# A chain of cross-attention layers on one core: another model behind the planned order, expert tiles in pairs, and zero rows written later

## Chip, core and metric

The kernel runs on one core of one Trainium2 chip. The metric is the device time of one execution in microseconds, as the median of several runs; less is better. A profile is one further execution, taken with the hardware profiler. The engines are TensorE (PE, matmuls and transposes; its weight loads are PEld), VectorE (DVE), ScalarE (ACT), GpSimd (POOL) and SyncE (SP, which here only issues transfers). ScalarE and GpSimd issue transfers too.

## What is computed

64 sequences of 128 x 128 float32 (`x`) and a context of 64 x 77 x 128 go through four layers. Layers 0 and 1 are single-head attentions without weight matrices (below called the front part). Layer 2 has self-attention, cross-attention with 16 heads of 8, and a mixture of experts; layer 3 has causal self-attention, cross-attention and a feed-forward part. Layer 2's experts are the part that the change touches:

```python
def _fuse_moe(x, ln_g, ln_b, rw, rb, fc1_w, fc1_b, fc2_w, fc2_b):   # E = 8, K = 2, DFF = 512
    h = _ln(x, ln_g, ln_b)
    logits = h @ rw.T + rb
    vals, idx = jax.lax.top_k(logits, K)
    gates = jax.nn.softmax(vals, axis=-1)
    hf = h.reshape(N, D)
    h1 = jax.nn.gelu(jnp.einsum('nd,efd->enf', hf, fc1_w) + fc1_b[:, None, :], approximate=False)
    eo = jnp.einsum('enf,edf->end', h1, fc2_w) + fc2_b[:, None, :]
    gathered = eo[idx_f, jnp.arange(N)[:, None], :]
    mixed = (gathered * gates_f[..., None]).sum(axis=1).reshape(x.shape)
    return x + mixed

x = _L0_xattn_ref(ctx_1024, x, ...)
x = _L1_xattn_ref(x, ctx_1024, ctx_1024, ...)
x = _L2_xattn_ref(x, ctx_1024, ...)
x = _L3_xattn_ref(x, ctx_1024, ...)
```

## The kernel before

**Tiles and sets.** The 64 sequences are taken four at a time: 16 batches, t = 0 to 15. Two batches (SG = 2, 1024 rows) make a set, of which there are 8. `front` (L974) does layers 0 and 1 of a batch, `middle` layer 2's two attentions, `router` the choice of two experts for each row, `dispatch` the places of a set's rows sorted by expert, and 16 scatters on GpSimd's queue (L1289) that write them into a DRAM tensor `sent[i]`. The rows of an expert fill whole tiles of 128, so a set has NT = 23 tiles, some rows of which no scatter writes. These must hold something finite, and so `sent[i]` is filled with zeros first (L700). `experts` reads the tiles in chunks of NL = 3 (7 chunks of 3 and one of 2), fetches each tile's expert weights by its number (L1326, L1327, on SP's queue, three buffers `we`, one tile ahead), and writes the answers to `answered[i]`. `gather` fetches each row's two answers (L1396), and `attention3` and `forward` do layer 3.

**An expert's tile.** One bf16 matmul with the bias parts and a mask (L1360), four float32 matmuls with the first weights (L1365), all into one PSUM tile `bank`; one Gelu on ScalarE over 128 x 512 (L1370); four matmuls with the second weights into another bank (L1375); and a copy on VectorE (L1376). ScalarE keeps one table of functions at a time. Gelu and Exp (L872, the softmaxes of the 16-head attentions) are in different ones, and the compiler puts an ACT_TABLE_LOAD between them.

**PSUM.** Three buffers `bank` (128 x 512 float32), used by nearly everything; one `banks` of four times that, for scores; one `po`, for the sums over keys.

**An attention tile.** Scores of one sequence into `banks` (L853 for the causal mask, L860); per half a maximum (L869) and a difference (L871) on VectorE and Exp on ScalarE (L872); eight transposes of the probabilities into two banks (L882), each copied by ScalarE (L883); sums over keys with narrow matmuls (L890), a copy (L941), a transpose (L899) and a division (L902, L903).

**The order.** It comes from two planners that run when the program is built. Each part above is a generator that yields before a piece of work the tiles that it needs. `Conductor` keeps a modelled time for each engine and lets that generator go on whose next piece can begin first (`begin`, with an age and a random blur from the plan; `ranks` break ties). The order of instructions so written is the program order, in which buffers are handed out. `Rehearsal` then takes all instructions with their dependencies and sorts those of TensorE, ScalarE, VectorE and GpSimd anew by a list schedule over modelled durations (`run`), and `apply` makes that order binding. In `run`, ScalarE puts off an instruction that would load a table by up to PATIENCE = 3000 ns if another is ready (`instead`). `run` also models TensorE's clock: in windows of WINDOW = 3413 ns it adds up TensorE's modelled work, and a window below a share BUSY makes the next one slow, with durations doubled. SP's queue keeps the program order. `tile_xattn_chain` rehearses each of four PLANS and builds the one with the least modelled length. A plan has a seed, the order in which an attention's four streams are added (`parts`), the batches that use the second of two lanes (`second`), the ranks, and a factor `slow` on TensorE's modelled time in `Conductor`. `Conductor` and `Rehearsal` each have a `cost` of their own.

**The start.** `load(0)` and `load(1)` on SP's queue; constants on ScalarE's queue (L579 to L601: columns, rows, fc1, fc2, matrices, router, biases, feed-forward weights); zeros for all eight sets on SP's queue (L690 to L701); and constants made on VectorE and TensorE (L615 onwards).

Of the kernel before, what the change touches and what calls it, by code (L numbers as in the profile page):

```python
# [40 lines left out]
    dict(age=2000.0, blur=300.0, seed=0, parts=(2, 3, 1, 0), second=(1, 3, 5), ranks=(2, 1, 0, 0, 0, 3), slow=1.2),  # L41
    dict(age=2000.0, blur=300.0, seed=527369, parts=(2, 0, 1, 3), second=(1, 3, 5), ranks=(2, 1, 0, 0, 2, 3), slow=1.2),
    dict(age=2000.0, blur=200.0, seed=622144, parts=(0, 1, 2, 3), second=(1, 3), ranks=(2, 1, 0, 0, 3, 3), slow=1.2),
    dict(age=2300.0, blur=200.0, seed=815169, parts=(3, 2, 0, 1), second=(1, 3), ranks=(2, 1, 0, 0, 0, 3), slow=1.2),
# [3 lines left out]
BUSY = (0.54, 0.88)  # L48
# [28 lines left out]

class Conductor:
# [7 lines left out]
    def __init__(self, block, bufs, plan):  # L86
        self.block, self.seen, self.bufs = block, 0, bufs
        self.age, self.blur, self.chance = plan["age"], plan["blur"], random.Random(plan["seed"])
        self.slow = plan["slow"]
        self.pe, self.table = 0.0, None  # L90
        self.busy, self.made, self.read, self.tiles = {}, {}, {}, {}
        self.streams = []
# [46 lines left out]
    def cost(self, i):  # L139

        kind = type(i).__name__
        sizes = [1.0]
        for o in list(i.ins) + list(i.outs):
            ap = getattr(o, "bass_ap", None)
            if ap is not None:
                size = 1.0
                for _, n in list(ap.ap)[1:]:
                    size *= n
                sizes.append(size)
        n, engine = max(sizes), i.engine.name  # L150
        if kind == "InstMatmult":
            n = sizes[1]
            if i.is_transpose:
                t = 0.85 * n
            elif "16" in str(i.ins[0].bass_ap.dtype):
                t = 0.43 * n
            else:
                t = 1.8 * n
            if i.tile_size is not None and 32 in tuple(i.tile_size):
                t *= 0.3  # L160
            return self.slow * t, self.slow * t + 160.0
        if "DMA" in kind:
            t = 950.0 if engine == "Pool" else 350.0
            return t, t + 2600.0
        if engine == "Pool":
            t = max(1000.0, 2.4 * n + 40.0)
            return t, t + 80.0
        if engine == "Activation":
            t = 80.0 + 0.83 * n
            if kind == "InstActivation":  # L170
                func = str(i.func)
                if "Exp" in func or "Gelu" in func:
                    if func != self.table:
                        t, self.table = t + 1283.0, func
                t += 100.0
            return t, t + 100.0
        t = 70.0 + 1.05 * n
        return t, t + 85.0

# [13 lines left out]
    def follow(self):  # L193

        instructions = self.block.instructions
        for i in instructions[self.seen :]:
            if "PoolBoundary" in type(i).__name__:
                continue
# [4 lines left out]
            for tensor in names[0]:  # L203
                t = max(t, self.made.get(tensor.name, 0.0))
            for tensor in names[1]:
                t = max(t, self.read.get(tensor.name, 0.0))
                tag = tensor.name.rsplit("_", 1)[0]
                if tag in self.bufs and tensor.name not in self.made:
                    t = max(t, self.free(tag))
                    self.tiles.setdefault(tag, []).append(tensor.name)  # L210
            keeps, takes = self.cost(i)
# [12 lines left out]
class Rehearsal:  # L224
# [3 lines left out]

    ENGINES = ("PE", "Activation", "DVE", "Pool")

    def __init__(self, block, slots):
        self.nodes = [i for i in block.instructions if "PoolBoundary" not in type(i).__name__]
# [59 lines left out]
    def cost(self, i, table):  # L292

        kind, engine, sizes, spaces, scalars = type(i).__name__, i.engine.name, [1], set(), 0
        aps = [[o.bass_ap for o in group if getattr(o, "bass_ap", None) is not None] for group in (i.ins, i.outs)]
        for ap in aps[0] + aps[1]:
            size = 1
            for _, n in list(ap.ap)[1:]:
                size *= n
            sizes.append(size)  # L300
            spaces.add(str(ap.tensor.space))
        n = max(sizes)
        scalars = sum(size == 1 for size in sizes[1:])
        if kind == "InstMatmult":
            n = sizes[1]
            if i.is_transpose:
                t = 0.85 * n
            elif "16" in str(aps[0][0].dtype):
                t = 0.42 * n
            else:  # L310
                t = 1.79 * n
            if i.tile_size is not None and i.tile_size[0] == 32:
                t = 0.237 * t + 30.0
            elif i.tile_size is not None and i.tile_size[1] == 32:
                t *= 0.315
            return t, t + 160.0, table
        if "DMA" in kind:
            t = 950.0 if engine == "Pool" else 360.0
            return t, t + 2600.0, table
        if engine == "Pool":  # L320
            t = 990.0 + 0.5 * n
            return t, t + 40.0, table
        if engine == "Activation":
            t = 165.0 + 0.833 * n
            if kind == "InstActivation":
                t += 90.0 * min(scalars, 2)
                func = str(i.func)
                if ("Exp" in func or "Gelu" in func) and func != table:
                    t, table = t + 1283.0, func
            return t - 98.0, t, table  # L330
        t = 150.0 + 1.04 * n + 60.0 * min(scalars, 2)
        if kind in ("InstTensorScalarPtr", "InstTensorCopy") and len(aps[0]) - scalars == 1 and len(spaces) == 1:
            t -= 0.52 * n
        if kind == "InstReciprocal":
            t += 40.0
        return t - 85.0, t, table

    def run(self):
# [15 lines left out]
        window, worked, over, slow = 0.0, 0.0, 0.0, False  # L354
        for k in range(len(nodes)):
            if not missing[k]:
                heapq.heappush(later[engine[k]], (0.0, k))
# [48 lines left out]
        for _ in nodes:  # L406
# [8 lines left out]
            keeps, takes, table = self.cost(nodes[k], table)  # L415
            if e == "PE":
                if any(name not in has for name in begins[k]):
                    keeps, takes = keeps + 80.0, takes + 80.0
                while t >= window + WINDOW:
                    slow = worked < BUSY[slow] * WINDOW  # L420
                    window, worked, over = window + WINDOW, over, 0.0
                if slow:
                    keeps, takes = 2.0 * keeps, takes + keeps
                inside = min(keeps, max(window + WINDOW - t, 0.0))
                worked, over = worked + inside, over + keeps - inside
# [49 lines left out]
    def apply(self, tc):  # L475
        for e in self.ENGINES:
# [23 lines left out]
def tile_xattn_chain(tc: tile.TileContext, *args: bass.AP):  # L500

    lengths = []
    for plan in PLANS:
        nc = bacc.Bacc("TRN2", target_bir_lowering=False, num_devices=1)
        copies = [nc.dram_tensor(a.tensor.name, a.shape, a.dtype, kind="ExternalInput").ap() for a in args]
        try:
            with tile.TileContext(nc) as scratch:
                lengths.append(perform(scratch, plan, *copies).length)
# [3 lines left out]
    plan = PLANS[lengths.index(min(lengths))]  # L512
    perform(tc, plan, *args).apply(tc)
# [3 lines left out]
def perform(  # L517
    ctx: ExitStack,
    tc: tile.TileContext,
    plan: dict,  # L520
    x: bass.AP,
# [37 lines left out]
    def bank():  # L559
        return ps1.tile([P, 512], F32, tag="bank", name="bank")  # L560

    def banks():
        return ps4.tile([P, 4, 512], F32, tag="banks", name="banks")
# [49 lines left out]
    byf_ps = bank()  # L613
# [56 lines left out]
    b1_ps = bank()  # L670
# [22 lines left out]
    zero = work.tile([P, NL, P], F32, tag="ye", name="zero", bufs=2)  # L693
    V.memset(zero, 0.0)
    for i in range(n_sets):
        sent.append(dram.tile([NT * P, P], F32, name=f"sent{i}"))
        answered.append(dram.tile([NT * P, P], F32, name=f"answered{i}"))
        for k in range(0, NT, NL):
            nl = min(NL, NT - k)
            nc.sync.dma_start(  # L700
                out=sent[i][k * P : (k + nl) * P].rearrange("(a p) d -> p a d", p=P), in_=zero[:, :nl]  # L701
# [34 lines left out]
    conductor = Conductor(nc.cur_bb.bb, {"bank": 3, "banks": 1, "po": 1}, plan)  # L736
# [567 lines left out]
    def experts(i):  # L1304
# [36 lines left out]
        for k in range(0, NT, NL):  # L1341
# [11 lines left out]
            for a in range(nl):  # L1353
                if k + a + 1 < NT:
                    load_weights(k + a + 1)
                we = weights.pop(0)
                yield room(xT, we, "bank", h1=1)
                held["h1"] += 1
                ps = bank()
                T.matmul(  # L1360
                    ps.rearrange("p (c q) -> p c q", c=NC), lhsT=b1s, rhs=bc(se["picks"][:, k + a, :], 2, P),
                    start=True, stop=False,
                )
                for c in range(NC):
                    T.matmul(  # L1365
                        ps[:, c * P : (c + 1) * P], lhsT=we[:, 0, c, :], rhs=xT[:, a * P : (a + 1) * P],
# [236 lines left out]
```

## Time and profile before

| | |
|---|---|
| median of 3 runs | 3008.31 us (3007.69, 3008.31, 3015.28) |
| the profiled execution | 3017.55 us |
| its span, first to last instruction | 3015.8 us |
| mean granted TensorE clock | 0.930 |
| instructions | 59018 |
| ACT_TABLE_LOADs, 1283 ns each | 319: 146 at L1370, 134 at L872, 39 elsewhere |
| DMA | 180.79 MB, mean 60 GB/s |

A line of a group reads: line of the kernel, engine, operation, output <- inputs, partitions x elements, count | busy time in us, mean ns of one | idle time of the engine just before them, and what ended most of it. Two of the largest groups and the parts of the page on the DMA queues:

```profile
L869 DVE TENSOR_REDUCE m<-banks 128x8 f32<-128x616 f32 (+1 forms) x512 | 512.8, 1002 | 273.1 <-PE banks L860 272.6
L882 PE MATMUL bank<-ident,pr 128*128 128x128 f32 (+1 forms) x4096 | 614.5, 291 | 105.7 <-ACT pr L872 38.0
...
we<-in_moe_w_dram SPq DMA_DIRECT2D x368, 256.0 KB
sent<-zero SPq DMA_DIRECT2D x56, 192.0 KB
```

A float32 matmul of the code shows as two MATMULs, a transpose as one. Matmuls overlap, so that eight in a row take less than eight times the mean of one.

### The profile page before, as it was taken

The numbers are of one execution on the slowest core, as the hardware profiler recorded it, in microseconds if no ns is written. First come the engines' busy times: TensorE is split into PE (matmuls) and PEld (weight loads), VectorE is DVE, ScalarE is ACT, GpSimd is POOL, SyncE is SP. The second block draws the span as 40 slices with busy tenths as digits, with TensorE's granted clock in tenths as the row PEclk, the third lists the DMA queues.
The fourth block names the chain that finished last, engine by engine and source line by source line (L and its number), as shares of the span: only waits on it lengthen the run. The fifth ranks groups of instructions, "written<-read, shape, count | busy, mean of one in ns | idle before, by whom it ended". The sixth has DMA issues, their size and how long they took to land. (4 is left out here: it accounts for less than half of the span.)

```text
span 3015.8 us, 59018 instructions
## 1 busy us (share of the span) xinstructions
PE 2526.9 (84%) x22732; PEld 1834.6 (61%) x22797; DVE 2114.6 (70%) x5412; ACT 1992.9 (66%) x3032; POOL 521.7 (17%) x506
## 2 busy tenths in 40 slices
PE   3687788788789987899879988889888989799987
PEld 2455566566566655666556665566655666566655
DVE  3788867666777776677667768677676667666675
ACT  1465567577677866777668775677756787677764
POOL 0111210320041103111040111301132001400210
PEclk9887888898989989999899999999988999999998
DMA  7000031331122211212122110222112121221100
GB/s 223 11 9 12 21 94 62 106 93 57 61 86 64 74 47 58 76 55 64 41 85 63 57 55 17 85 66 61 39 43 69 50 65 57 86 71 56 42 8 8
DMA packets 168256, 180.79 MB, mean 60 GB/s; under 512 B 15708, under 2 KB 111784, under 8 KB 167848
## 3 DMA queue, kind: packets, MB, share of 16 engines
q1 hardware_dynamic: 157936, 157.03, 16.9%
q0 software_dynamic: 8192, 16.79, 1.9%
q8 instruction: 180, 2.95, 0.4%
q10 hardware_dynamic: 1848, 3.19, 0.4%
q14 instruction: 100, 0.82, 0.1%
HBM read 133.54 MB, written 43.42 MB: 59 GB/s over the span
## 5 line engine op out<-in xcount | busy, mean ns | idle before, releaser
L869 DVE TENSOR_REDUCE m<-banks 128x8 f32<-128x616 f32 (+1 forms) x512 | 512.8, 1002 | 273.1 <-PE banks L860 272.6
L882 PE MATMUL bank<-ident,pr 128*128 128x128 f32 (+1 forms) x4096 | 614.5, 291 | 105.7 <-ACT pr L872 38.0
L883 ACT COPY pT<-bank 128x512 f32<-128x512 f32 (+1 forms) x1024 | 556.4, 585 | 199.0 <-PE bank L882 196.5
L882 PEld LDWEIGHTS bank<-ident,pr 128*128 128x128 f32 (+1 forms) x4096 | 478.0, 151 | 270.2 <-issue 66.9
L872 ACT ACTIVATE pr<-pr 128x616 f32<-128x616 f32 (+1 forms) x512 | 447.8, 887 | 169.7 <-DVE pr L871 166.0
L871 DVE TENSOR_TENSOR pr<-banks,m 128x616 f32<-128x616 f32 (+1 forms) x512 | 514.6, 1005 | 31.7 <-PE bank L882 11.6
L750 POOL TENSOR_TENSOR rs<-ve,mhalf 128x4 f32<-128x4 f32 (+1 forms) x160 | 165.9, 1037 | 1798.4 <-DVE ve L748 1682.9
L890 PE MATMUL po<-pT,vpad 77*32 77x128 f32 (+1 forms) x8192 | 388.4, 283 | 8.6 <-ACT oT L941 4.8
L860 PE MATMUL banks<-KX,QT 32*128 32x308 f32 (+1 forms) x2048 | 308.4, 588 | 53.2 <-DVE pr L871 40.4
L890 PEld LDWEIGHTS po<-pT,vpad 77*32 77x32 f32 (+1 forms) x8192 | 219.9, 110 | 137.6 <-issue 99.3
L1375 PE MATMUL bank<-we,he 128*128 128x128 f32 x1472 | 224.0, 298 | 24.5 <-ACT he L1370 10.2
L1375 PEld LDWEIGHTS bank<-we,he 128*128 128x128 f32 x1472 | 194.4, 205 | 54.1 <-issue 13.8
L1365 PEld LDWEIGHTS bank<-xT,we 128*128 128x128 f32 x1472 | 204.6, 201 | 20.1 <-issue 11.4
L1365 PE MATMUL bank<-xT,we 128*128 128x128 f32 x1472 | 205.5, 284 | 0.0
L1370 ACT ACT_TABLE_LOAD x146 | 187.3, 1283 | 23.4 <-PE bank L1365 21.0
L1396 POOL DMA_INDIRECT ans<-answered,rows_i x128 | 127.3, 994 | 304.8 <-DMA answered<-ye 135.2
L860 PEld LDWEIGHTS banks<-KX,QT 32*128 32x128 f32 x2048 | 98.5, 193 | 126.2 <-issue 82.2
L872 ACT ACT_TABLE_LOAD x134 | 171.9, 1283 | 3.5 <-DVE pr L871 1.2
L766 PE MATMUL bank<-ident,xh 128*128 128x128 f32 (+1 forms) x448 | 92.7, 323 | 89.4 <-DVE xh L753 74.5
L1370 ACT ACTIVATE he<-bank 128x512 f32<-128x512 f32 x184 | 109.9, 597 | 78.7 <-PE bank L1365 76.7
L1289 POOL DMA_INDIRECT sent<-xm,rows_i x128 | 125.5, 981 | 192.3 <-DVE picks L1279 111.6
L766 PEld LDWEIGHTS bank<-ident,xh 128*128 128x128 f32 (+1 forms) x448 | 61.3, 159 | 119.0 <-DVE xh L753 48.2
(242 smaller groups left out, 3687.4 us busy)
## 6 DMA issues: line engine op xcount, KB each, us to landing
we<-in_moe_w_dram SPq DMA_DIRECT2D x368, 256.0 KB
sent<-zero SPq DMA_DIRECT2D x56, 192.0 KB
xe<-sent SPq DMA_DIRECT2D x56, 192.0 KB
answered<-ye SPq DMA_DIRECT2D x56, 192.0 KB
X<-in_x_dram SPq DMA_DIRECT2D x16, 256.0 KB
later_x<-x3b SPq DMA_DIRECT2D x16, 256.0 KB
x<-later_x SPq DMA_DIRECT2D x16, 256.0 KB
out_dram<-y SPq DMA_DIRECT2D x16, 256.0 KB
```

What stands on the lines that cost most here:

```text
L750: G.tensor_tensor(rs[:p], ve[:p], mhalf[:p], ALU.pow)
L766: T.transpose(ps[:, b * p : (b + 1) * p], src[:, b, :], ident[:p, :p])
L860: T.matmul(sc[:, g, : NJ * nk].rearrange("q (j k) -> q j k", j=NJ), lhsT=QT[part, b, :], rhs=KX[part, :, b, :nk], start=not is_causal, sto ...
L869: recent["max"] = V.tensor_reduce(m, scores, AX.X, ALU.max)
L871: V.tensor_tensor(pr, scores, bc(m, 3, nk), ALU.subtract)
L872: S.activation(pr, pr, AF.Exp, scale=DH**-0.5)
L882: T.transpose(pt[:nk, j * P : (j + 1) * P], pr[:, i, j, :], ident)
L883: S.copy(pT[:nk, i].rearrange("k j q -> k (j q)"), pt[:nk])
L890: T.matmul(po[32 * g : 32 * g + 32, half * P : half * P + P], lhsT=vp[:nk, b, 4 * half + g, 32 * k : 32 * k + 32], rhs=pT[:nk, g // 2, g % ...
L1365: T.matmul(ps[:, c * P : (c + 1) * P], lhsT=we[:, 0, c, :], rhs=xT[:, a * P : (a + 1) * P], start=False, stop=c == NC - 1,)
L1370: S.activation(he.rearrange("p c q -> p (c q)"), ps, AF.Gelu)
L1375: T.matmul(eo[:, 0:P], lhsT=he[:, c, :], rhs=we[:, 1, c, :], start=c == 0, stop=c == NC - 1)
```

## The change

1. **Constants of the planners.** PLANS are four others, BUSY is other, and KEPT, UNREAD and SPARE are new.
2. **One cost function.** `cost` (that of `Rehearsal`, with a term for the bytes of a transfer) serves both planners. In `Conductor`, an instruction that isn't TensorE's and reads a `bank`, `banks` or `po` tile begins only after that tile's earlier readers.
3. **Clock model.** `Rehearsal.run` weighs each matmul's time by the share of the 128 x 128 array that it fills (`fullness`) before comparing it with BUSY. It can also plan fillers: matmuls whose result is not read, ahead of the first use of a PSUM tile, where the share of use in the last window is below KEPT. `perform` takes their numbers as `fills` and issues them in `bank()` and `banks()`.
4. **Experts in pairs.** Within a chunk, the first matmuls of two tiles come first, into two banks, then their two gelus, then the second matmuls of each. A chunk of 3 is a pair and a single.
5. **Zero rows.** The zeros are a row of a constant that is no longer needed (`3c_bo`, already added to `be1`), broadcast along the tiles, and `clear(i)` writes those of set i after the front part of the set's first batch.

```diff
 PLANS = [
-    dict(age=2000.0, blur=300.0, seed=0, parts=(2, 3, 1, 0), second=(1, 3, 5), ranks=(2, 1, 0, 0, 0, 3), slow=1.2),
-    dict(age=2000.0, blur=300.0, seed=527369, parts=(2, 0, 1, 3), second=(1, 3, 5), ranks=(2, 1, 0, 0, 2, 3), slow=1.2),
-    dict(age=2000.0, blur=200.0, seed=622144, parts=(0, 1, 2, 3), second=(1, 3), ranks=(2, 1, 0, 0, 3, 3), slow=1.2),
-    dict(age=2300.0, blur=200.0, seed=815169, parts=(3, 2, 0, 1), second=(1, 3), ranks=(2, 1, 0, 0, 0, 3), slow=1.2),
+    dict(age=2000.0, blur=200.0, seed=949959, parts=(0, 1, 2, 3), second=(1, 3, 5), ranks=(2, 1, 0, 0, 0, 1), slow=1.05),
+    dict(age=2000.0, blur=200.0, seed=984142, parts=(0, 1, 2, 3), second=(1, 3, 5), ranks=(2, 1, 0, 0, 0, 1), slow=1.05),
+    dict(age=2000.0, blur=200.0, seed=787737, parts=(0, 1, 2, 3), second=(1, 3, 5), ranks=(2, 1, 0, 0, 0, 1), slow=1.05),
+    dict(age=1700.0, blur=200.0, seed=167013, parts=(0, 1, 2, 3), second=(1, 3, 5), ranks=(2, 1, 0, 0, 0, 1), slow=1.05),
 ]
...
-BUSY = (0.54, 0.88)
+BUSY = (0.45, 0.79)
+KEPT = (0.0, 0.0)
+UNREAD = 225.0
+SPARE = 150.0
...
+def fullness(i):
+
+    moving, held = [o.bass_ap for o in i.ins if getattr(o, "bass_ap", None) is not None][:2]
+    size = 1
+    for _, n in list(held.ap)[1:]:
+        size *= n
+    share = list(moving.ap)[0][1] / P * size / P
+    if i.tile_size is not None and 32 in tuple(i.tile_size):
+        share *= 4.0 if i.tile_size[0] == 32 else 3.2
+    return min(share, 1.0)
...
             for tensor in names[0]:
                 t = max(t, self.made.get(tensor.name, 0.0))
+                if tensor.name.rsplit("_", 1)[0] in self.bufs and i.engine.name != "PE":
+                    t = max(t, self.read.get(tensor.name, 0.0))
...
-            keeps, takes = self.cost(i)
+            keeps, takes, self.table = cost(i, self.table)
+            if i.engine.name == "PE":
+                keeps, takes = self.slow * keeps, self.slow * takes
...
             if e == "PE":
...
+                new = [name for name in begins[k] if name not in has]
+                if len(new) == 1 and new[0] in self.numbers and shared(t) < KEPT[slow]:
+                    at, _ = slot(k)
+                    at = max(at, free[e]) + 60.0
+                    one = UNREAD * (1.0 + slow)
+                    count = int(min((t - at - SPARE) / one, 12.0))
+                    if count > 0:
+                        self.fills[self.numbers[new[0]]] = count
...
+                longer = work(t, keeps, fullness(nodes[k]))
+                keeps, takes = longer, takes + longer - keeps
...
-    zero = work.tile([P, NL, P], F32, tag="ye", name="zero", bufs=2)
-    V.memset(zero, 0.0)
     for i in range(n_sets):
         sent.append(dram.tile([NT * P, P], F32, name=f"sent{i}"))
         answered.append(dram.tile([NT * P, P], F32, name=f"answered{i}"))
+
+    zero = row["3c_bo"]
+    V.memset(zero, 0.0)
+
+    def clear(i):
+
         for k in range(0, NT, NL):
             nl = min(NL, NT - k)
             nc.sync.dma_start(
-                out=sent[i][k * P : (k + nl) * P].rearrange("(a p) d -> p a d", p=P), in_=zero[:, :nl]
+                out=sent[i][k * P : (k + nl) * P].rearrange("(a p) d -> p a d", p=P), in_=bc(zero, 1, nl)
             )
...
-            for a in range(nl):
-                if k + a + 1 < NT:
-                    load_weights(k + a + 1)
-                we = weights.pop(0)
-                yield room(xT, we, "bank", h1=1)
...
+            for first in range(0, nl, 2):
+                pair = []
+                for a in range(first, min(first + 2, nl)):
+                    if k + a + 1 < NT:
+                        load_weights(k + a + 1)
+                    we = weights.pop(0)
+                    yield room(xT, we, "bank", h1=1)
+                    held["h1"] += 1
+                    ps = bank()
...
+                    pair.append((a, we, ps))
+
+                after = []
+                for a, we, ps in pair:
+                    he = work.tile([P, NC, P], F32, tag="h1", name="he", bufs=4)
+                    S.activation(he.rearrange("p c q -> p (c q)"), ps, AF.Gelu)
+                    after.append(he)
+                for (a, we, ps), he in zip(pair, after):
+                    yield he, "bank"
+                    held["h1"] -= 1
+                    eo = bank()
+                    for c in range(NC):
+                        T.matmul(eo[:, 0:P], lhsT=he[:, c, :], rhs=we[:, 1, c, :], start=c == 0, stop=c == NC - 1)
+                    V.tensor_copy(ye[:, a], eo[:, 0:P])
...
             yield from front(states[t])
             fronted.add(t)
+            if t % SG == 0:
+                clear(t // SG)
```

## The prediction

> **What bounds the kernel now.** I read the page first (busy shares, clock, chain), then the busy time in stretches, then the first 60 us instruction by instruction, then the groups and the waits around the experts' gelus.
>
> ```profile
> PE 2526.9 (84%) x22732; PEld 1834.6 (61%) x22797; DVE 2114.6 (70%) x5412; ACT 1992.9 (66%) x3032; POOL 521.7 (17%) x506
> PEclk9887888898989989999899999999988999999998
> PE 12%; DVE 6%; ACT 3%; issue 2%; POOL 1%; DMA 1%; POOLq 0%; DVEq 0%; ACTq 0%; SPq 0%
> ```
>
> No engine is full. TensorE is nearest, with 489 us idle in a span of 3015.8. The chain is traced back over only about a quarter of the span (its shares add up to some 25%), and in it TensorE has 12 of 25 parts, VectorE 6, ScalarE 3. The mean granted clock is 0.930, and the records know full and half speed alone, so 2 x 0.07 x 3015.8 = 422 us ran at half clock; with TensorE 84% busy, half of 354 us, 177 us, is what that cost its matmuls at most.
>
> ```profile
> 0.00:100.00 100.00, 36.67 (x159) 26.65 (x160) 49.59 (x201) 20.96 (x32) 12.91 (x20) 1.00 0.60 176
> 100.00:200.00 100.00, 76.51 (x635) 54.70 (x634) 74.81 (x175) 56.45 (x91) 9.91 (x9) 0.78 0.02 7
> 1400.00:1600.00 200.00, 168.32 (x1448) 122.42 (x1442) 133.04 (x352) 130.88 (x196) 43.31 (x42) 0.92 0.21 64
> 2600.00:2800.00 200.00, 184.07 (x1782) 134.63 (x1795) 134.22 (x281) 157.19 (x235) 16.21 (x14) 1.00 0.23 70
> ```
>
> After the start, length, PE, PEld, DVE, ACT, POOL, clock, DMA share and GB/s. The first 100 us are a serial start. After that the stretches differ: 164 to 184 busy in 200 us for the ten from 600 to 2600 and the one after, at clocks from 0.91 to 1.00. The work is the same in kind; what differs is how the streams lie beside each other. So the kernel is bound by its **order**: who is late varies from moment to moment. From 100 to 2900 us TensorE is busy 2402.6, so 397 us idle are there to be had in principle.
>
> **Part 1: the zero rows leave the start.** The 64 transfers at L700 are issued in one run on SP's queue and carry 56 x 192 + 8 x 128 KB = 11.8 MB.
>
> ```profile
> 2.72 52.78 SPq L700 DMA_DIRECT2D sent<-zero  x64
> ...
> 11.84 0.02 ACT L587 MOVE_SHAPE mat_sb<-in_mats_dram  x1 [11.84 <-DMA sent<-zero]
> ...
> 23.34 0.40 PE L671 MATMUL bank<-ident,moe_b_sb 128*32 128x128 f32 x1 [12.35 <-DMA moe_b_sb<-in_moe_b_dram]
> ...
> 29.40 0.28 DVE L744 BATCH_NORM_STATS2 st<-C 77x6 f32<-77x128 f32 x1
> ```
>
> ScalarE's constant loads stand behind them, TensorE's transposes behind the load that lands at 23.3, VectorE's constants behind those, and the first front part starts at 29.40. From 0 to 55 us the DMA engines move 239 to 321 GB/s, so they are full. Without the zeros the first loads are the rows (1.5 MB), X and C twice (0.8), the matrices (1.0) and ff (0.5): 3.9 MB / 280 GB/s = 14 us, 9.5 us before 23.3. By the other bound, ScalarE's own issues: the rows land at 9.81 and the ten issues after them take 5.1 us (0.33 to 1.26 each), then 3.0 us of flight (20.73 to 23.74): 17.9, 5.4 us earlier. Between the two: **-8** (-5 to -14, the far end if the rows land sooner too). What follows is serial, so the end moves with it.
>
> Where the zeros go: 8 transfers on SP's queue after the first front part of each of 8 sets, 1.5 MB each: 8 x 0.36 us of issue and 5.3 us at 280 GB/s. Their readers are the scatters at L1289. In this trace set 0's front ends near 80 us and its scatter starts at 363; set 7's near 2035 and 2557; the shortest lead of the eight is some 270 us. SP's queue runs in order, and a clear can stand behind a weight load that waits for its buffer, 24.5 us at the longest; the lead covers it. Behind a clear, weight loads are 2.9 us late; TensorE waited 0.3 us in all for weights (L1365). **0**; without that cover, 2.9 + 5.3 + about 3 us of landing on each of 8 sets, 90 us.
>
> **Part 2: gelus in pairs.** ScalarE swaps tables between Gelu and Exp.
>
> ```profile
> L1370 ACT ACT_TABLE_LOAD x146 | 187.3, 1283 | 23.4 <-PE bank L1365 21.0
> L872 ACT ACT_TABLE_LOAD x134 | 171.9, 1283 | 3.5 <-DVE pr L871 1.2
> L1370 ACT ACTIVATE he<-bank 128x512 f32<-128x512 f32 x184 | 109.9, 597 | 78.7 <-PE bank L1365 76.7
> PE bank L882 <- ACT he L1370: 14.9, 17, 1.4
> PE bank L1375 <- ACT he L1370: 10.2, 12, 2.2
> ```
>
> 146 of 184 gelus bring a load. A chunk has 3 tiles, so it becomes one pair and one single; the last chunk of 2 is one pair: 7 x 2 + 1 = 15 groups a set, 120 in all, with 64 pairs. At the old rate, 0.79 a group, that is 95 loads; at one each 120; I take 108. So 38 gelu loads go, and as many Exp loads on the way back: 76 x 1.283 = 97 us of ScalarE (64 to 131). How much is on the path? At least none; at most all 97. ScalarE's share of the chain, 3 in 25, is the nearest row: 97 x 0.12 = **-12**.
>
> In this trace a load starts at 57.57, when the ACTIVATE before it ends (56.77 + 0.78), so a swap takes its 1.28 us and no more. The Trainium skill's page "ScalarE: Activation LUTs", section "What ACT_TABLE_LOAD costs", puts 1380 ns of drain on top of the 1283 ns. By that page's 2.66 us the 76 loads would be an estimated 202 us of ScalarE and the path term -24 in place of -12; the trace shows no such drain, so it stays out.
>
> The price is in PSUM. There are three buffers called bank; the first tile of a pair now keeps its one while the second's nine matmuls run, 1.4 us when close together, and then ScalarE, in order, does load and two gelus, 1.28 + 2 x 0.6 = 2.5 us, in which one bank is left and its eviction (L883) stands behind the gelus. One such stall today:
>
> ```profile
> 1547.81 1.04 PE L882 MATMUL bank<-ident,pr 128*128 128x128 f32 x8
> 1550.00 1.13 PE L882 MATMUL bank<-ident,pr 128*128 128x128 f32 x8 [1.15 <-ACT he L1370]
> ```
>
> Bounds: 0, if scores and po (no bank, 1.1 us a burst each) fill the time; 64 x 1.15 = 74 us if every pair stalls so. The waits on the gelu seen now sum to some 30 us over 184 gelus, 0.16 each; nearest to that, at 0.12 a pair more: **+8**.
>
> The granted clock was 1.00 from 2600 to 2800, with experts running all the time, so bursts through three banks do not of themselves slow it here. The Trainium skill's page "TensorE: Matmul & The Clock Gate", section "A second HAM failure mode: psum-queue depth-cycling", speaks against this part: cycling through PSUM banks gives short idles, and the clock is throttled again and again. If each pair cost one window of 3.4 us (that page's figure) at half speed, an estimate is 64 x 1.7 = 109 us, and by it the sum would come out slower than before.
>
> **Part 3: the model and the plans.** No instruction is added: a filler is planned only where the use is below KEPT, and that is 0.0 and 0.0, which no share is below. What changes is the order on all four engines, from the first yield on: one cost function for both planners, reads of a PSUM tile by other engines counted in turn, DMA time that grows with size, matmuls of small tiles weighed by the array they fill, thresholds 0.45 and 0.79, four new plans. The trace can't price an order that it doesn't have. Upper bound of the gain: the 397 us idle and the 177 of clock. Its size I take from the spread of the 200 us stretches: 164 to 184 has a deviation of about 3%; over the 14 of the middle 3%/sqrt(14) = 0.8%, 25 us, is what one draw of an order of this kind is worth to either side. The old plans are a best of four as well, but by a model that knew neither transfer time nor the array's use; I count 1.5 deviations: **-38** (from +38 to -130, a third of the idle time).
>
> **Sum.** The profiled run took 3017.55 us (span 3015.8 and 1.75 around it): -8 + 0 - 12 + 8 - 38 = -50, so 2967.5. That run is 9.2 us above the median of 3008.31; on the median, **2958**.
>
> **Rivals.**
> A. *The bank ring starves* (slower). One mechanism, in the experts' stretches from 400 to 2820 us: during load and two gelus TensorE finds no free bank. At 1.15 us for each of 64 pairs, +74, with the order worth nothing: 3008 - 8 - 12 + 74 = 3062. It decides from (8 + 12 + 38) / 64 = 0.9 us a pair on. For it: the row at 1550.00, and that ScalarE is the emptier of every bank but few. Against: stalls of 0.16 us per gelu today, and the planner knows the three slots. 0.22.
> B. *The order is only another draw*: parts 1 and 2 alone, 3008 - 12 = 2996, give or take 25. For it: nothing in the trace measures the new model. Against: 397 us idle that a truer clock can aim at. 0.16.
> C. *The order recovers a third of the idle time*: 3008 - 12 - 130 = 2866, or up to 2915 with a quarter of it. For it: the stretch from 2600 on shows 92% busy at full clock, with experts in it. Against: the early stretches, 76 to 80% at 0.78 to 0.85, have few streams whatever the plan. 0.17.
> The forecast, 2915 to 2990 about 2958, has 0.45.
>
> **Range and chances.** 2880 to 3040 holds the forecast, B, most of C and the nearer part of A; one in ten lies beyond each end. No change means within 0.3%, 2999 to 3017: the three runs differ by 0.25%. Faster: 0.45 + 0.17 + half of B, 0.70; same 0.07, from B's middle and A's edge; slower 0.23.
>
> **What would show it.** Part 1: no zeros before the first front part, L744 near 21 us, full DMA for some 15 us only, and the scatters never waiting on a clear. Part 2: 95 to 120 gelu loads and some 240 in all, against 319; ScalarE about 1,895 us busy; waits of bank matmuls on the gelu below 40 us (A: near 100). Part 3: TensorE idle near 440 us, clock 0.94. Wrong if the idle time grew though table loads fell: then the banks or the order took it.

## The result, and the profile after

| | before | after |
|---|---|---|
| median, same chip, 6 runs each | 3010.19 us | 2978.34 us |
| ratio of the times, 95% interval | | 0.9898 (0.9874 to 0.9923) |
| profiled execution, span | 3015.8 us | 2977.9 us |
| TensorE busy, idle in the span | 2526.9, 489 | 2552.0, 426 |
| mean granted clock | 0.930 | 0.921 |
| ACT_TABLE_LOADs | 319 | 253 |

The change makes the kernel 1.0% faster, 31 us (23 to 38 by the interval), where 50 was forecast. On the page of the changed kernel, the rows that answer to those shown of before:

```profile
PE 2552.0 (86%) x22797; PEld 1832.1 (62%) x22797; DVE 2118.1 (71%) x5412; ACT 1906.1 (64%) x2966; POOL 520.6 (17%) x506
PEclk9888799789989998999899998998989999999999
L1416 ACT ACT_TABLE_LOAD x113 | 145.0, 1283 | 18.1 <-PE bank L1407 16.1
L1416 ACT ACTIVATE he<-bank 128x512 f32<-128x512 f32 x184 | 107.2, 596 | 59.7 <-PE bank L1407 58.2
```

ScalarE lost 87 us of work, as the pairs were to bring, but TensorE has more busy time than before, not less, and the granted clock fell. 2 x 0.079 x 2977.9 = 470 us ran at half clock, 48 more than before; half of 48, 24 us, is an estimate of what that costs. TensorE's busy time grew by 25 us, of which some 7 are only recorded more fully: 65 of the 22797 matmuls are missing from the trace of before (65 at its mean of 0.11 us). Its idle time fell by 63 us. 63 - 25 = 38 is the whole difference of the two spans. The stretches (start and end, length, busy PE, PEld, DVE, ACT, POOL, granted clock, DMA share, GB/s) say where, first those of the changed kernel and then two of before:

```profile
0.00:100.00 100.00, 48.23 (x257) 33.70 (x258) 60.23 (x215) 31.93 (x47) 13.13 (x20) 0.98 0.61 176
100.00:200.00 100.00, 80.96 (x698) 54.29 (x701) 78.30 (x188) 55.64 (x93) 10.91 (x10) 0.81 0.02 7
300.00:400.00 100.00, 66.30 (x522) 47.30 (x525) 63.42 (x184) 46.39 (x73) 24.38 (x24) 0.73 0.16 52
1000.00:1200.00 200.00, 175.86 (x1490) 125.98 (x1482) 131.94 (x350) 124.75 (x193) 42.31 (x41) 0.90 0.21 65
1400.00:1600.00 200.00, 170.27 (x1570) 118.27 (x1568) 151.53 (x392) 126.45 (x206) 48.68 (x46) 0.91 0.17 51
2600.00:2800.00 200.00, 187.21 (x1766) 135.06 (x1765) 129.98 (x279) 147.42 (x226) 22.11 (x22) 0.97 0.23 68
```

```profile
300.00:400.00 100.00, 75.48 (x631) 53.42 (x632) 77.31 (x219) 52.23 (x86) 25.41 (x25) 0.80 0.13 42
1000.00:1200.00 200.00, 164.34 (x1494) 120.45 (x1488) 136.95 (x357) 134.52 (x205) 34.32 (x33) 0.92 0.18 57
```

The first 100 us are fuller by 11.6 us of TensorE. After that there is no stretch in which the gain sits: some are fuller (1000 to 1200 at 175.9 against 164.3), one is emptier (300 to 400 at 66.3 against 75.5, at a clock of 0.73). That is what another order looks like, not one stall removed. The start of the changed kernel, in order of time:

```profile
3.35 0.02 ACT L623 MOVE_SHAPE mat_sb<-in_mats_dram  x1 [3.35 <-DMA col_sb<-in_cols_dram]
...
9.23 0.29 DVE L784 BATCH_NORM_STATS2 st<-C 77x6 f32<-77x128 f32 x1 [0.43 <-DMA C<-in_context_dram]
...
14.93 0.40 PE L707 MATMUL bank<-ident,moe_b_sb 128*32 128x128 f32 x1 [5.45 <-DMA moe_b_sb<-in_moe_b_dram]
...
16.79 2.68 SPq L740 DMA_DIRECT2D sent<-row_sb  x5
...
35.97 26.72 SPq L740 DMA_DIRECT2D sent<-row_sb  x40
...
38.13 0.69 DVE L1082 TENSOR_TENSOR ca<-bank,row_sb 128x512 f32<-128x512 f32 x1 [7.94 <-PE bank L1080]
```

and the last of these rows in the kernel before:

```profile
51.87 0.69 DVE L1042 TENSOR_TENSOR ca<-bank,row_sb 128x512 f32<-128x512 f32 x1 [8.00 <-PE bank L1040]
```

The biases land at 14.9 and not at 23.3, and the front part reaches `ca` at 38.13, where it was at 51.87. But the zero rows are **not** written behind each set's front part: all 64 transfers leave between 16.8 and 62.7 us. The section on the kernel before says that SP's queue keeps the program order; that order is not the one of the code: in the program as built, all 64 clears stand ahead of the fourth batch's loads. The framework below the planners has put each transfer as early as its operands allow, and a clear needs only its zeros (a wait added to the clears moves them, as the run with late clears shows). What holds them back now is their source, a row of a constant that has to land and be added to another before it is set to zero.

### The profile page after: what moved, and what is told of

The parts are those of the page before. It is cut to its first block, busy times and chain, and to the rows that moved or that the text cites. A ratio compares the mean times of both kernels' runs of the same rounds, so it can differ in the third digit from the quotient of the medians.

```text
span 2977.9 us, 58985 instructions
## 1 busy us (share of the span) xinstructions
PE 2552.0 (86%) x22797; PEld 1832.1 (62%) x22797; DVE 2118.1 (71%) x5412; ACT 1906.1 (64%) x2966; POOL 520.6 (17%) x506
## 5 line engine op out<-in xcount | busy, mean ns | idle before, releaser
L909 DVE TENSOR_REDUCE m<-banks 128x8 f32<-128x1024 f32 (+1 forms) x512 | 512.8, 1002 | 301.2 <-PE banks L900 300.1
L912 ACT ACTIVATE pr<-pr 128x1024 f32<-128x1024 f32 (+1 forms) x512 | 450.9, 887 | 199.9 <-DVE pr L911 196.5
L911 DVE TENSOR_TENSOR pr<-banks,m 128x1024 f32<-128x1024 f32 (+1 forms) x512 | 514.6, 1005 | 20.4 <-PE bank L922 0.9
L790 POOL TENSOR_TENSOR rs<-ve,mhalf 128x4 f32<-128x4 f32 (+1 forms) x160 | 164.3, 1027 | 1998.9 <-DVE ve L788 1949.4
L930 PE MATMUL po<-pT,vpad 77*32 77x128 f32 (+1 forms) x8192 | 398.4, 286 | 7.0 <-ACT pT L923 4.0
L900 PE MATMUL banks<-KX,QT 32*128 32x308 f32 (+1 forms) x2048 | 320.7, 609 | 52.3 <-DVE pr L911 41.0
L1423 PE MATMUL bank<-we,he 128*128 128x128 f32 x1472 | 212.0, 293 | 11.6 <-ACT he L1416 3.6
L1416 ACT ACT_TABLE_LOAD x113 | 145.0, 1283 | 18.1 <-PE bank L1407 16.1
L981 ACT COPY oT<-po 128x256 f32<-128x256 f32 x256 | 94.6, 370 | 84.7 <-PE po L930 82.9
L942 DVE RECIPROCAL rs<-bank 128x16 f32<-128x16 f32 x256 | 63.2, 248 | 105.8 <-PE bank L939 105.1
```

What stands on the lines that cost most here:

```text
L790: G.tensor_tensor(rs[:p], ve[:p], mhalf[:p], ALU.pow)
L900: T.matmul(sc[:, g, : NJ * nk].rearrange("q (j k) -> q j k", j=NJ), lhsT=QT[part, b, :], rhs=KX[part, :, b, :nk], start=not is_causal, sto ...
L909: recent["max"] = V.tensor_reduce(m, scores, AX.X, ALU.max)
L911: V.tensor_tensor(pr, scores, bc(m, 3, nk), ALU.subtract)
L912: S.activation(pr, pr, AF.Exp, scale=DH**-0.5)
L930: T.matmul(po[32 * g : 32 * g + 32, half * P : half * P + P], lhsT=vp[:nk, b, 4 * half + g, 32 * k : 32 * k + 32], rhs=pT[:nk, g // 2, g % ...
```

## The experiments

Twelve kernels ran, on three chips; each ratio is to the kernel before on the same chip. The kernel before takes 3013.77 us on the chip of the first four (part 1, its source alone, pairs without the model, model without pairs) and 3004.49 us on that of the next four (the three seeds and the old Conductor). The late clears, the two kernels with the old clock and the one with both planners old ran on a chip on which it takes 3094.65 us. So the ratios are compared, and an expectation in us is read as a ratio to 3010 (2994 us is 0.9947).

### Part 1 alone, and its source alone

```diff
-    zero = work.tile([P, NL, P], F32, tag="ye", name="zero", bufs=2)
+    zero = row["3c_bo"]
...
+                clear(t // SG)
```

> The kernel before with part 1 alone (zeros from the row constant, written by clear(i) after the front parts), old planners and plans; the engines' orders differ from before only in a few neighbouring places. Theory of the prediction: the serial start moves about 14 us forward (the profile of the changed kernel shows the first front part 13.7 us earlier, -8 was forecast) and the end moves with it: 2994 to 3002 us. Rival: what is won at the start is given back where the streams wait for each other later: 3007 to 3013. In the changed kernel's profile all 64 zero transfers still leave between 17 and 63 us, so the transfers should not be seen spread over the span here either.

The second kernel has the first two of these lines, with the 64 transfers left where they were in the code:

> The kernel before with two lines changed: the zeros are the memset row constant, broadcast, but all 64 transfers stay where they were written, at the start. Theory formed on the changed kernel's profile: the place in the code does nothing, since the transfers are issued as soon as their source is ready; what helps is that the source now is a row that must land first, which keeps the zeros behind the constants. Then it is as fast as part 1 as a whole, within 5 us: 2994 to 3002. Rival: the place counts, and this one stays at 3005 to 3013.

Part 1: 3002.76 us, ratio 0.9968 (0.9955 to 0.9981), so 9.6 us are won (5.7 to 13.5). Source alone: 3005.05 us, 0.9980 (0.9961 to 0.9998). As ratios the expected 2994 to 3002 us are 0.9947 to 0.9973, so the first is inside; the second lies between that range and the rival's, which begins at 3005 (0.9983), and the time alone does not decide there. The traces do. In the first 60 us of the two, first part 1 as a whole:

```profile
11.12 17.28 SPq L704 DMA_DIRECT2D sent<-row_sb  x24
...
16.11 0.40 PE L671 MATMUL bank<-ident,moe_b_sb 128*32 128x128 f32 x1 [5.89 <-DMA moe_b_sb<-in_moe_b_dram]
...
22.07 0.28 DVE L748 BATCH_NORM_STATS2 st<-C 77x6 f32<-77x128 f32 x1
...
44.63 0.69 DVE L1046 TENSOR_TENSOR ca<-bank,row_sb 128x512 f32<-128x512 f32 x1 [8.02 <-PE bank L1044]
```

and then the source alone:

```profile
11.76 43.83 SPq L700 DMA_DIRECT2D sent<-row_sb  x64
...
22.16 0.28 DVE L744 BATCH_NORM_STATS2 st<-C 77x6 f32<-77x128 f32 x1
...
44.69 0.69 DVE L1042 TENSOR_TENSOR ca<-bank,row_sb 128x512 f32<-128x512 f32 x1 [8.00 <-PE bank L1040]
```

The same start within 0.1 us, 7.2 us ahead of before at `ca`: up to there the source does all of it, and the place in the code nothing. At the end the means of the two (12 executions each) are 2.4 us apart, give or take 2.4 (95%), so whether the place is worth anything there is open. The other 6.5 us of the 13.7 in the changed kernel come with its order, which takes the statistics of the first batch (9.23) ahead of VectorE's last constants.

### The clears made to leave late

```diff
-            nc.sync.dma_start(
+            d = nc.sync.dma_start(
...
+            if "max" in recent:
+                wait(d.ins, recent["max"].ins, "late")
```

> The changed kernel with its own plan, each set's zero transfers (from the second set on) made to wait for the latest maximum of an attention before them, so that they really leave behind the front parts; the order of the four engines is the same by the model (2832.0 us in both). If the zeros that fill the DMA engines from 17 to 63 us still hold something up there: 2968 to 2975. Theory: nothing waits for them any more, 2975 to 2982. Rival: behind the weight loads they make the scatters or the experts wait: 2985 or more.

0.9877 (0.9849 to 0.9904), against 0.9898 (0.9874 to 0.9923) of the changed kernel: no difference that these runs show. Its median lies in the range of the first hypothesis (0.9860 to 0.9884) and its interval reaches over the theory's (to 0.9907), so the time does not decide between them. Its clears do leave late; the first of them on SP's queue, and the front part of the first batch:

```profile
198.34 5.89 SPq L737 DMA_DIRECT2D sent<-row_sb  x8
403.52 5.03 SPq L737 DMA_DIRECT2D sent<-row_sb  x8
636.67 4.55 SPq L737 DMA_DIRECT2D sent<-row_sb  x8
```

```profile
38.04 0.69 DVE L1081 TENSOR_TENSOR ca<-bank,row_sb 128x512 f32<-128x512 f32 x1 [7.94 <-PE bank L1079]
```

With 8 transfers in the first 63 us in place of 64 the front part reaches `ca` at 38.04, against 38.13, so up to there the zeros hold nothing up. The cover that the prediction named for late clears holds: no scatter waits on one, and no loss shows; the third hypothesis (2985 us or more, 0.9917) falls.

### Pairs without the new model

The kernel before with parts 1 and 4 of the change (zeros and pairs); planners and plans old.

```diff
-            for a in range(nl):
+            for first in range(0, nl, 2):
+                pair = []
+                for a in range(first, min(first + 2, nl)):
```

> The kernel before with part 1 and the pairs, but the old planners and old plans. Theory of the prediction: pairs are worth -4 us on top of part 1 (-12 of table loads, +8 of banks): 2990 to 2998. Rival A (banks starve): 3030 or more. Rival that the pairs carry most of the gain: 2975 to 2985, so near the changed kernel without its model. Gelu loads 100 to 120 in each case.

2999.99 us, 0.9958 (0.9940 to 0.9977), inside the theory's range (0.9934 to 0.9960) and 3 us below part 1 alone. The two intervals overlap; by the means of 10 and 12 executions on the one chip the difference is 3.7 us, give or take 3.4 (95%), so it stands at the edge of what they can tell. Its page against that of part 1 alone, one row of this kernel and then one of the other:

```profile
PE 2538.4 (85%) x22797; PEld 1827.8 (61%) x22797; DVE 2120.3 (71%) x5412; ACT 1910.8 (64%) x2966; POOL 519.4 (17%) x506
```

```profile
PE 2530.6 (84%) x22797; PEld 1829.7 (61%) x22797; DVE 2115.2 (70%) x5412; ACT 1992.4 (66%) x3032; POOL 519.6 (17%) x506
```

82 us of ScalarE went, and some 3 us of time followed. TensorE is busy 8 us longer, at a lower granted clock: 0.923 to 0.930 in the ten executions, against 0.930 to 0.933 in the twelve of part 1 alone.

### The new model without pairs

The changed kernel with its four plans, but one tile after the other as before; of the four plans the planner then takes seed 787737.

> The changed kernel with the experts' tiles one by one as before; model, plan list and zeros as changed (of the four plans the planner then picks another, seed 787737). Theory of the prediction (the order is the larger part, pairs are worth little): 2975 to 2985. Rival (the gain is in pairs, the model gives nothing): 2990 to 3000. Third: the four plans were found with pairs in the program and are four arbitrary orders without them; then the time is that of an unselected order, 3000 to 3040.

3042.93 us, 1.0095 (1.0064 to 1.0127): slower than before, and the third of the three hypotheses (3 us above its range, and as a ratio inside it). Taken alone this could still mean that pairs and model need each other. The next runs decide that.

### Seeds that were looked for, and one that was not

In each of these the list of plans holds one plan, with another seed and all else as in the first plan:

```diff
 PLANS = [
-    dict(age=2000.0, blur=200.0, seed=949959, parts=(0, 1, 2, 3), second=(1, 3, 5), ranks=(2, 1, 0, 0, 0, 1), slow=1.05),
...
+    dict(age=2000.0, blur=200.0, seed=1, parts=(0, 1, 2, 3), second=(1, 3, 5), ranks=(2, 1, 0, 0, 0, 1), slow=1.05),
```

> The changed kernel with one plan, the first of its four with the seed 1, which nobody looked for; its modelled length is 2920 us, against 2832 for the plan that the changed kernel builds. Selection theory (the gain beyond the start is that of a seed found by the model, and chip time follows the modelled length): 3030 to 3070. Rival (the new model makes better orders with any seed, as the sum's -38 for the order supposes of the model itself): 2965 to 2995. Second rival (the chip does not follow the model, the order is a draw): anywhere about 3010, give or take 30.

> The same with seed 1010, the shortest by the model of some 80 seeds tried in a row; modelled 2831 us, the same as the changed kernel's 2832. Selection theory: the same time as the changed kernel, 2970 to 2990. Draw rival: about 3010, give or take 30, with no relation to 2978.

The third has no pairs, and a seed that was searched in that form:

> The changed kernel without pairs, with a seed that was looked for in that form too (1034, shortest of some 80, modelled 2845 us). Selection theory: 2985 to 3000, so most of the 43 us between the changed kernel and the one without pairs and with its left-over plans comes back. Rival (pairs and model need each other): 3020 or more.

| kernel | modelled length | time | ratio |
|---|---|---|---|
| changed, seed 949959 | 2832 | 2978.34 | 0.9898 (0.9874 to 0.9923) |
| changed, seed 1010 | 2831 | 2979.98 | 0.9925 (0.9900 to 0.9950) |
| no pairs, seed 1034 | 2845 | 2981.28 | 0.9927 (0.9901 to 0.9953) |
| no pairs, seed 787737 | 2884 | 3042.93 | 1.0095 (1.0064 to 1.0127) |
| changed, seed 1 | 2920 | 3023.91 | 1.0071 (1.0029 to 1.0114) |

With a seed that nobody looked for, the changed kernel is slower than before, pairs, zero rows and new model included; the rival that the model makes better orders with any seed (2965 to 2995) falls. With a searched seed it is as fast without pairs as with them, so the rival that pairs and model need each other falls too. The modelled length separates the three fast from the two slow, though not by the amount: seeds 1010 and 1, on one chip, are 89 us of the model and 44 us of the chip apart, and the two slow ones are not told apart. As ratios all three forecasts of the selection theory hold (1.0066 to 1.0199, 0.9867 to 0.9934, 0.9917 to 0.9967).

The draw rival, 3010 give or take 30 (0.990 to 1.010), holds each of the three times as well; no run alone excludes it. Against it stands the row of kernels: those of the new Conductor with a seed that the planner ranks short, two of them further down, are five in this document, at 0.985 to 0.993, and the two whose seed was not searched for in their form stand at 1.007 and 1.010. Were the order a mere draw, that split would come once in 21 times (in 15, if the two with seed 949959 count as one).

Among 48 seeds in a row (1 to 48) the planner's own lengths are, in us:

```text
                               mean   deviation   shortest
changed kernel                 2934.9    66.2      2848.2
changed kernel, no pairs       2920.5    30.0      2854.7
old planners, zeros and pairs  2882.7    43.5      2815.0
old planners, zeros            2891.1    24.9      2833.2
```

The two upper rows and the two lower are by different models and can't be compared with each other. By the one model pairs lengthen the mean by 14 us, by the other they shorten it by 8, neither beyond what 48 draws can tell; by both they widen the spread.

The groups of table loads in the kernel without pairs and with seed 1034:

```profile
L1407 ACT ACT_TABLE_LOAD x140 | 179.6, 1283 | 20.5 <-PE bank L1402 18.2
L909 ACT ACT_TABLE_LOAD x128 | 164.2, 1283 | 2.2
```

303 loads in all, 50 more than in the changed kernel, at a time that can't be told from that of seed 1010, which has 229.

### Which planner does it

The old Conductor (its own costs, the old plans' settings) below the new Rehearsal, with a searched seed:

```diff
-            keeps, takes, self.table = cost(i, self.table)
-            if i.engine.name == "PE":
-                keeps, takes = self.slow * keeps, self.slow * takes
+            keeps, takes = self.cost(i)
```

> The changed kernel with the old first planner: Conductor's own old costs and the old plans' settings (age 2000, blur 300, ranks with the experts last), the new Rehearsal, and a seed looked for in the same way (1059, modelled 2848 us). Selection theory: 2985 to 3000, from the modelled length alone. Rival (the new Conductor is what helps): 3000 or more. If it falls below 2970, the old Conductor is the better one.

3019.44 us, 1.0051 (1.0018 to 1.0084). The selection theory missed this one by 19 us, and the rival (3000 or more) has it: with 2848 modelled us it is slow, where 2845 without pairs were fast on the same chip, so a short modelled length is no promise.

The other way round, Conductor and plan as changed and Rehearsal's clock as before:

```diff
-BUSY = (0.45, 0.79)
+BUSY = (0.54, 0.88)
...
-                longer = work(t, keeps, fullness(nodes[k]))
+                longer = work(t, keeps, 1.0)
```

> The changed kernel with its own plan and Conductor, but with Rehearsal's clock as before: every matmul counts as filling the array, thresholds 0.54 and 0.88. By this model, too, this plan is the shortest of the four. Theory (the first planner's sequence and its seed carry the gain, the clock that follows the array's use does not): 2970 to 2995. Rival (that clock is what makes the order better): 3000 or more.

0.9851 (0.9821 to 0.9882), below the theory's range (0.9867 to 0.9950) and not slower than the changed kernel. On the same chip the changed kernel with late clears has 0.9877 (0.9849 to 0.9904), which is not told from it. With a seed searched by that clock:

> Conductor as changed, Rehearsal's clock as before, and the seed that is shortest by that model among some 80 (1031, modelled 2801 us, against 2802 for the changed kernel's plan by the same model). Selection theory: 2970 to 2995, as the changed kernel. Draw rival: about 3010, give or take 30. Below 2965 it would be the fastest of all.

0.9899 (0.9872 to 0.9926), inside the theory's range and as fast as the changed kernel, yet on one chip 11 us slower than the run above, give or take 8, though the model has the two within 0.5 us of each other. That is how far two orders lie apart that the model calls equal. And both planners old, with a searched seed:

> Both planners as before, with pairs and zeros as changed, and a seed looked for among some 140 in the same way (1003, modelled 2811 us by the old model; the old plan with pairs was 2832 by it and took 3000 on the chip). Selection theory: the 21 us of the model show on the chip, 2975 to 2990. Rival (the new Conductor is needed, as the run with the old one and a searched seed, 3019, suggests): 3000 or more.

0.9929 (0.9908 to 0.9951), inside the theory's range (0.9884 to 0.9934). The rival (3000 us or more, a ratio from 0.997) falls: with zeros, pairs and a searched seed the old planners come within 0.3% of the changed kernel's 0.9898, and the intervals overlap. Against the changed kernel with late clears, on the same chip, they are 0.5% slower, and those intervals don't overlap. Two orders of equal modelled length lie nearly as far apart, so that difference does not show a share of the new planners by itself. Nor do the 21 modelled us against the old plan with pairs show clearly: 0.9958 and 0.9929, with intervals that overlap.

Five of these kernels can be compared by nearly one model, since the two `Rehearsal`s with the old clock differ only in the term for the bytes of a transfer: zeros alone 2846, with pairs 2832, with seed 1003 2811, and the two with the old clock 2802 and 2801. Their ratios are 0.9968, 0.9958, 0.9929, 0.9851 and 0.9899: in the same order, but for the last two.

No run here is clearly faster than the changed kernel; the lowest ratio is that with the old clock and the changed kernel's own plan.

## Why the prediction was right, and where it was off

**Sign and mechanism.** Faster was forecast at 0.70, and the time lies inside the range and inside the forecast's own band of 2915 to 2990. It lies inside rival B's band too (2996 give or take 25), so the time alone does not separate the two. The kernel is bound by its order, as the first reading said: three independent orders (seeds 949959 and 1010, and 1034 without pairs) give 0.990 to 0.993, and two others 1.007 and 1.010, with the same work but for the table loads. TensorE's idle time was forecast near 440 us and is 426.

**Part 1, -8 forecast.** -9.6 measured (-5.7 to -13.5); the statistics of the first front part were to begin near 21 us, and begin at 22.07 with part 1 alone. The two bounds, 14 us by bytes and 17.9 by ScalarE's issues, hold between them the landing of the biases in that kernel, 16.1. What failed is the sentence that puts the zeros on SP's queue behind the first front part of each set: they leave at once, up to 62.7 us, and "full DMA for some 15 us only" was wrong with it. That the gain came all the same was luck: the source chosen for the zeros is a row that lands late enough, and the prediction did not reckon with that. Leaving later than they do brings the zeros neither a gain nor a loss that the runs show.

**Part 2, -12 + 8 = -4 forecast.** -3 measured, at the edge of what the runs tell from nothing. The counts came out: 113 loads at the gelu (95 to 120), 253 in all (240), ScalarE at 1906 us (1,895). The two terms can't be told apart by these runs. Rival A, the starved ring of banks, is out. It needed waits of TensorE on the gelu near 100 us; they fell from 30 us to 17 in the changed kernel, whose three largest are:

```profile
PE bank L922 <- ACT he L1416: 8.9, 15, 1.3
PE bank L1423 <- ACT he L1416: 3.6, 6, 1.0
PE bank L939 <- ACT he L1416: 1.7, 2, 0.8
```

With pairs and the old planners the granted clock fell from 0.932 to 0.926, and the time did not grow. The Trainium skill's page "TensorE: Matmul & The Clock Gate", section "A second HAM failure mode: psum-queue depth-cycling", which was weighed against the pairs, would have the clock fall so, but the 109 us estimated from that page did not come. Whether the pairs' use of the banks lowered the clock is not shown: each kernel has an order of its own, and without pairs (seed 787737) it is 0.924 to 0.928, with pairs (seed 1010) 0.928 to 0.938. The drain that the page "ScalarE: Activation LUTs" adds to a table load ("What ACT_TABLE_LOAD costs") can't be tested by the time here, since ScalarE's work hardly reaches it.

**Part 3, -38 forecast.** This is the term that was mis-sized: -31 in all, less -9.6 and -3, leaves about -18. The step was "I count 1.5 deviations" of 25 us each. No run measures either factor. The 25 us were read from the stretches; two seeds of the changed kernel are 44 us apart on one chip, and by the planner the deviation is 66 us, so 25 was not too wide. And the reason given for 1.5 deviations, a model that knows the array's use, is not what pays: with the old clock the same plan is as fast (0.9851), and the granted clock, forecast at 0.94, fell to 0.921. What pays in these runs is a sequence that was searched for and that the planner ranks short, with the old Conductor under the new Rehearsal as the exception. The kernel before starts from such a sequence too: its plan has 2846 us by the old model, and of the 48 seeds above only two are shorter; how its seed was found is not known here. So what part 3 gained is one well-ranked order over another. Rival B, "only another draw", was nearer the truth in its reason than the forecast, but for the search.

**Small slips of the working.** The four loads of part 1 add up to 3.8 MB, not 3.9; the lower end of ScalarE's saving is 67 us, not 64 (26 loads, twice); a quarter of the idle time would bring rival C to 2897, not 2915. None moves the sum.

**Open.** Whether the new Conductor has a share. The old one gave 1.0051 under the new Rehearsal and 0.9929 under the old, both with searched seeds; with one seed each, spread and cause can't be told apart.

## What to carry to other kernels

Where a planner with a seed makes the order, compare a change with several seeds, found with the same effort on both sides: here one seed against another moved the time by 1.5% on one chip, more than the whole change. Work taken off an engine that is 66% busy bought next to nothing here (82 us of table loads, some 3 us of time): look first whether the engine that sets the end waits for it. And look in the trace for where a moved transfer really leaves: its operands, not its place in the code, decided that here.

## What was not expected of the hardware

In the kernel before, ScalarE's issue of the matrices waited until 11.84 us, and the profile names one of SP's zero transfers as what ended the wait; with the zeros behind the constants it went on at 3.35. That looks like one queue holding up another, but the program asks for it: as built, the transfers of both queues take eight completion semaphores in turn, and each waits for the one before it on the same semaphore. That of the matrices comes behind the first zero transfer in the kernel before, and behind the columns in the changed one, as the two rows say. So the 64 zeros took the semaphores of ScalarE's loads as well as the DMA engines' time; which of the two cost more is not shown.

Chips differ. The kernel before took 3010 us on one chip and 3095 on another, 2.8% apart, more than the whole change; its granted clock there was 0.917 to 0.922, against 0.926 to 0.937 on the two other chips of the experiments. All four traces from the slower chip hold waits that no instruction of the core ended ("remote"; the largest row of the run with late clears stands below), 78 to 121 us summed over the engines, and the other ten traces hold none. What they are, and whether they make the chip slower, is open. The one pair that can be compared, the changed kernel and the one that differs only in when its zeros leave, has 0.9898 and 0.9877 on the two.

```profile
ACT pT L922 <- remote: 50.3, 8, 14.0
```
